# Last layer of a four-layer graph network: inverse roots computed between the statistics of other blocks, the last five roots on ScalarE, and two blocks of edge counts loaded one layer ahead

## The chip, the cores and the metric

The kernel runs on one core of one Trainium2 chip. The metric is device time in microseconds (us); the median of several runs is compared. A profile of one execution is shown beside the times. In it PE is TensorE (matmul), PEld its weight loads, DVE is VectorE, ACT is ScalarE, POOL is GpSimd, and SP is SyncE, the engine that issues most DMAs here.

## The reference, cut to what matters

Four graph layers run one after the other over the same 3125 nodes with 128 features and 103125 edges. After each layer the result is added to its input and normalised over the features.

```python
x = _layernorm(x + _L0_gnn_ref(...))   # weighted sum over the edges, relu
x = _layernorm(x + _L1_gnn_ref(...))   # attention with four heads
x = _layernorm(x + _L2_gnn_ref(...))   # attention with softmax
x = _layernorm(x + _L3_gnn_ref(...))   # this one, below

agg = segment_sum(x[src], dst) / maximum(deg, 1)
h   = relu(agg @ w1_l + b1 + x @ w1_r)              # 128 -> 256
agg = segment_sum(h[src], dst) / maximum(deg, 1)
y   = sigmoid(agg @ w2_l + b2 + h @ w2_r)           # 256 -> 128

def _layernorm(x, eps=1e-5):
    m = mean(x); v = var(x)
    return (x - m) / sqrt(v + eps)
```

## The kernel before, in words

The nodes are laid out as 25 blocks of 128 (`NB = 25`, `P = 128`, `NP = 3200`). The edges have been turned into a dense matrix of counts in DRAM, `ctd`: 25 row blocks of 128 x 3200 bf16, 800 KB each. A segment sum is then a product of this matrix with the features, and the kernel streams the row blocks from DRAM and multiplies.

A scheduler in the framework sets the order of instructions on each engine from their dependencies and from the order in the program. A tile pool that is opened takes the addresses of pools closed before it, and its first writers wait for the readers of those. DVE and ACT work on the last stage is an exception: it stands in a `manual_schedule` block, where these two engines keep the order of the program. SP's queue is in order, so a DMA whose wait is not met holds those behind it.

**Layer 2** runs over two groups of blocks (`QG`, 13 and 12) and, in each, over the 25 row blocks; `scores(q, c)` loads a strip of counts into `ct2` (three buffers), multiplies, takes the exponential on ACT and multiplies by the counts on DVE. The pool `p3` is opened before layer 2 and stays open through layer 3. It holds `f_rdeg`, `f_rdr`, the tile `f_ct0` (row block 0 of the counts, which layer 3 needs first) and the inputs of layer 3's products, `ip0` to `ip6`. The load of `f_ct0` (L1429) is written in the program at step 12 of the second group; the scheduler has put it on SP's queue behind the first three loads of layer 2.

**Layer 3** has two passes over the counts. The first (L1486) takes row blocks 0 to 19 from `ct0` or from `counts(b)`, a pool of six buffers filled on SP (L1477), then the last five blocks per 512 columns with the dense products between. The second pass (`add2`, L1562) keeps eight accumulators in PSUM, one for each group of output blocks:

```python
GT = [(0, 4), (4, 4), (8, 4), (12, 4), (16, 4), (20, 2), (22, 2), (24, 1)]
```

Its last five row blocks are multiplied group by group, so that group 0 is complete first and group 7 last. Each complete group g then goes through these steps:

- `sigmoid(g)`: DVE scales each block's accumulator and adds the own term (L1580, one instruction per block), ACT takes the sigmoid of the whole group (L1583).
- `moments(g)`: DVE adds the layer's input (L1588, one instruction per group), then one `bn_stats` (L1591) and one `bn_aggr` (L1593) per block give mean and variance in `mv`.
- `normal(b0, n)`: DVE computes 1/sqrt(var + eps) for n blocks with thirteen small instructions, each fed by the one before it: `var`, `half`, `sd` (L1598 to L1602), three Newton steps of three instructions (L1605 to L1607), and `ms` (L1609). ACT then writes the n normalised blocks (L1615), and SP stores them (L1619, L1621 for the 53 rows of the last block).

`normal` is called for blocks 0 to 7 after the sigmoid of group 2, for 8 to 15 after group 4, for 16 to 19 after group 5, and for 20 to 24 at the end, where two of the five blocks are written by DVE (L1613).

Of the kernel before, what the change touches and what calls it, by code (L numbers as in the profile page):

```python
# [7 lines left out]
F32 = mybir.dt.float32  # L8
BF16 = mybir.dt.bfloat16
I32 = mybir.dt.int32  # L10
AF = mybir.ActivationFunctionType
OP = mybir.AluOpType
# [3 lines left out]
P = 128  # L16
N = 3125
NB = 25
NP = NB * P
# [11 lines left out]
EPS = 1e-5  # L31
# [472 lines left out]
GT = [(0, 4), (4, 4), (8, 4), (12, 4), (16, 4), (20, 2), (22, 2), (24, 1)]  # L504
# [4 lines left out]
def fast_path(  # L509
# [4 lines left out]
    nc = tc.nc  # L514
# [3 lines left out]
    ctd = dram.tile([NB, P, NP], BF16, name="f_ctd")  # L518
# [8 lines left out]
    x = cst.tile([P, NB, P], F32, name="f_x")  # L527
    deg = cst.tile([P, NB], F32, name="f_deg")
# [118 lines left out]
    for g in range(NG):  # L647
        eg = ep.tile([P, EW // 16, 3, 16], F32, name="eg", bufs=3)
        nc.gpsimd.indirect_dma_start(
            out=eg.rearrange("p a t k -> p (a t k)"), out_offset=None, in_=td,  # L650
# [204 lines left out]
    for b in range(NBT):  # L855
        ohd, ohc, wod, _ = cur
# [49 lines left out]
    r = xw  # L906
# [9 lines left out]
    lp = ctx.enter_context(tc.tile_pool(name="f_p12", bufs=1))  # L916
# [14 lines left out]
    def step():  # L931

        todo = [f for k, f in due if k <= now[0]]
        due[:] = [(k, f) for k, f in due if k > now[0]]
        for f in todo:
            f()
        now[0] += 1
# [115 lines left out]
    with ExitStack() as st:  # L1053
# [239 lines left out]
        for x_, (g, hp, c) in enumerate(items):  # L1293
            i0, n = IG[g]
# [29 lines left out]
    p3 = ctx.enter_context(tc.tile_pool(name="f_p3", bufs=1))  # L1324
    rdeg = p3.tile([P, NB], F32, name="f_rdeg")
    rdr = p3.tile([P, NP], F32, name="f_rdr")
    ct0 = p3.tile([P, NP], BF16, name="f_ct0")
    ips = {}

    def in_parts(lp, g, i):  # L1330
# [6 lines left out]
    scale = float(P) ** -0.5  # L1337
    with ExitStack() as st:
# [13 lines left out]
        def degrees():  # L1352

            nc.vector.tensor_scalar(rdeg, deg, 1.0, None, OP.max)
            nc.vector.reciprocal(rdeg, rdeg)
            rd_ = dram.tile([NB, P], F32, name="rd_")
            t = bank()
            nc.tensor.transpose(t[0:NB, 0:P], rdeg, ident)
            rt = l2.tile([NB, P], F32, name="rt")
            nc.scalar.copy(rt, t[0:NB, 0:P])  # L1360
            nc.sync.dma_start(rd_, rt)
            nc.sync.dma_start(rdr, bass.AP(tensor=rd_.tensor, offset=rd_.offset, ap=[[0, P], [1, NP]]))
# [58 lines left out]
        for x_, (q, c) in enumerate(items):  # L1421
            i0, n = QG[q]
            if c == 0:
                acc = [ap.tile([P, 512], F32, name=f"acc2_{k}") for k in range((n + 2) // 3)]
            step()
            if (q, c) == (0, 3):
                degrees()
            if (q, c) == (1, 12):
                nc.sync.dma_start(ct0, ctd[0])  # L1429
            if q == 0 and NB - 4 <= c < NB - 1:  # L1430
                a = split + (c - NB + 4) * 512
                turned_y(a, min(512, N - a))
            if x_ + 1 < len(items):
                scores(*items[x_ + 1])
            if c < NB - 2:
                for k in range(n):
                    products2(acc, q, c, k)
            elif c == NB - 1:
                for k0 in range(0, n, 3):
                    m = min(3, n - k0)  # L1440
                    for b in (NB - 2, NB - 1):
                        for k in range(k0, k0 + m):
                            products2(acc, q, b, k)
                for k0 in range(0, n, 3):
                    m = min(3, n - k0)
                    t = acc[k0 // 3][:, 0 : m * (P + 1)].rearrange("p (b d) -> p b d", d=P + 1)
                    z = cp.tile([P, 3], F32, name="z2")
                    nc.vector.tensor_scalar(z[:, 0:m], t[:, :, P], 1e-38, None, OP.max)
                    nc.vector.reciprocal(z[:, 0:m], z[:, 0:m])
                    for j in range(m):  # L1450
                        b = i0 + k0 + j
                        nc.vector.scalar_tensor_tensor(
                            r[:, b, :], t[:, j, 0:P], z[:, j : j + 1], x[:, b, :], OP.mult, OP.add
                        )
                finish2(q)
# [5 lines left out]
    with ExitStack() as st:  # L1461
        fp = st.enter_context(tc.tile_pool(name="f_fp3", bufs=1))
        cp = st.enter_context(tc.tile_pool(name="f_cp3", bufs=HB + 1))
        lp = st.enter_context(tc.tile_pool(name="f_lp3", bufs=2))
# [6 lines left out]
        for g in range(3, len(GB)):  # L1471
            b0, n = GB[g]
            ips[g] = in_parts(lp, g, x[:, b0 : b0 + n, :])

        def counts(b):
            ct = cp.tile([P, NP], BF16, name="ct3")
            nc.sync.dma_start(ct, ctd[b])  # L1477
            return ct
# [11 lines left out]
            return done  # L1490

        for b in range(NB - HB):
            ct = counts(b) if b else ct0
            for k in range(len(CN)):
                done = add1(ct, b, k)
            if 3 <= b < 17 and b % 2:
                with tc.issue_after(done.ins):
                    turned(ps, xT, *GB[(b - 3) // 2])
            if b == 18:

                sd = fp.tile([P, 1], F32, name="f_sumdeg")
                nc.vector.tensor_reduce(sd, deg, AX.X, OP.add)
                t = ps.tile([P, 512], F32, name="tr")
                nc.tensor.matmul(t[:, 0:1], ones, sd, start=True, stop=True)
                nc.vector.tensor_scalar(good[:, 2:3], t[:, 0:1], float(E), None, OP.is_equal)
                nc.vector.tensor_tensor(good[:, 3:4], good[:, 0:1], good[:, 1:2], OP.mult)
                nc.vector.tensor_tensor(good[:, 3:4], good[:, 3:4], good[:, 2:3], OP.mult)
                nc.vector.tensor_copy(flag, good[0:1, 3:4])
# [32 lines left out]
        for k in range(K + 3):  # L1541
            if k < K:
                for b in range(NB - HB, NB):
                    add1(last[b], b, k)
                c, n = CN[k]
# [22 lines left out]
        for b in range(NB - HB):  # L1568
            ct = counts(b)
# [3 lines left out]
        mv = fp.tile([P, NB, 2], F32, name="mv3")  # L1573
        sg = {}

        def sigmoid(g):
# [6 lines left out]
            nc.scalar.activation(t, t, AF.Sigmoid)  # L1583
            sg[g] = t

        def moments(g):
            b0, n = GT[g]
            nc.vector.tensor_tensor(r[:, b0 : b0 + n, :], sg[g], x[:, b0 : b0 + n, :], OP.add)  # L1588
            bs = lp.tile([P, 4, 6], F32, name="bs3")
            for j in range(n):  # L1590
                nc.vector.bn_stats(bs[:, j, :], r[:, b0 + j, :])  # L1591
            for j in range(n):
                nc.vector.bn_aggr(mv[:, b0 + j, :], bs[:, j, :])  # L1593

        def normal(b0, n, by_v=()):

            va = lp.tile([P, 8], F32, name="var3")[:, 0:n]
            nc.vector.tensor_scalar(va, mv[:, b0 : b0 + n, 1], EPS, None, OP.add)  # L1598
            half = lp.tile([P, 8], I32, name="half3")[:, 0:n]
            nc.vector.tensor_scalar(half, va.bitcast(I32), 1, None, OP.arith_shift_right)  # L1600
            sd = lp.tile([P, 8], F32, name="sd3")[:, 0:n]
            nc.vector.tensor_scalar(sd.bitcast(I32), half, -1.0, float(0x5F3759DF), OP.mult, OP.add)  # L1602
            t = lp.tile([P, 8], F32, name="newton")[:, 0:n]
            for _ in range(3):
                nc.vector.tensor_tensor(t, sd, sd, OP.mult)  # L1605
                nc.vector.scalar_tensor_tensor(t, t, -0.5, va, OP.mult, OP.mult)
                nc.vector.scalar_tensor_tensor(sd, t, 1.5, sd, OP.add, OP.mult)  # L1607
            ms = lp.tile([P, 8], F32, name="ms3")[:, 0:n]
            nc.vector.scalar_tensor_tensor(ms, mv[:, b0 : b0 + n, 0], -1.0, sd, OP.mult, OP.mult)  # L1609
            for j in range(n):  # L1610
                b = b0 + j
                if b in by_v:
                    nc.vector.tensor_scalar(x[:, b, :], r[:, b, :], sd[:, j : j + 1], ms[:, j : j + 1], OP.mult, OP.add)  # L1613
                else:
                    nc.scalar.activation(  # L1615
                        x[:, b, :], r[:, b, :], AF.Identity, bias=ms[:, j : j + 1], scale=sd[:, j : j + 1]
                    )
            m = min(n, NF - b0)
            nc.sync.dma_start(out[b0 * P : (b0 + m) * P, :].rearrange("(b p) d -> p b d", p=P), x[:, b0 : b0 + m, :])  # L1619
            if m < n:  # L1620
                nc.sync.dma_start(out[NF * P : N, :], x[0:NR, NF, :])  # L1621

        with tc.manual_schedule(engines={mybir.EngineType.DVE, mybir.EngineType.Activation}):
            for g in range(len(GT)):
                for b in range(NB - HB, NB):
                    add2(last[b], b, g)
                sigmoid(g)
                if g == 2:
                    normal(0, 8)
                elif g == 4:  # L1630
                    normal(8, 8)
                elif g == 5:
                    normal(16, 4)
                moments(g)
            normal(20, 5, (NB - 2, NB - 1))


@with_exitstack
# [39 lines left out]
```

## Time and profile before

| | |
|---|---|
| median of 3 runs | 1528.68 us (1528.14 to 1530.35) |
| the profiled execution, whole | 1528.75 us |
| its span in the profile | 1526.9 us |
| PE busy | 1391.9 us (91%) |
| DVE busy | 985.8 us (65%) |
| ACT busy | 910.6 us (60%) |
| last matmul ends | about 1505.2 us |
| last ACT instruction ends | about 1521.0 us |

The page of a profile shows, in its section 2, the busy share of each engine in 40 slices of the span, a digit for each slice: 9 is 90% or more. The timeline lists instructions in order of time: start, duration, engine, line of the program, operation, tiles, shapes and count; neighbours of one line are merged, and a bracket gives idle time before the instruction and what ended it. The table by windows gives the busy time of each engine in a stretch, the granted clock of TensorE, the mean busy share of the 16 DMA engines and the GB/s that they moved.

### The profile page before, as it was taken

To read this page: it belongs to the slowest core of one execution; us is meant where nothing else is said; L and a number is where in the kernel's file an instruction comes from. 1 tells how busy PE (TensorE), PEld (TensorE's weight loads), DVE (VectorE), ACT (ScalarE), POOL (GpSimd) and SP (SyncE) were. 2 spreads that over 40 slices of the span, in tenths; PEclk is the share of its full clock that TensorE was granted. 3 is DMA by queue.
4 is the path that set the end of the run, shared out by engine and by line. 5 is a ranking of instruction groups with operands and counts; after the bars stand their busy time and mean duration, and the time that the engine had idled before them with its cause. 6 is when DMAs were issued, how large, how long until landed. Compare 5 with 4: busy or idle time off the path is not lost. (4 is left out here: it accounts for less than half of the span.)

```text
span 1526.9 us, 35224 instructions
## 1 busy us (share of the span) xinstructions
PE 1391.9 (91%) x14858; PEld 1220.9 (80%) x14871; DVE 985.8 (65%) x1608; ACT 910.6 (60%) x1865; POOL 126.8 (8%) x162
## 2 busy tenths in 40 slices
PE   4899999999997987899989989899999999999994
PEld 3898999998997876889979979677777764458994
DVE  4999899999990489879978888544464451012006
ACT  2988778888882479878778677554465431023003
POOL 2000000000000023203212311300000000000000
PEclk9999999999998999999999999999999999999997
DMA  6387787887878633444434433332222227503551
GB/s 193 88 216 212 208 228 206 236 211 208 222 211 247 207 96 99 145 123 122 129 121 116 130 89 104 101 111 68 73 64 80 69 89 259 200 22 151 196 174 45
DMA packets 210337, 223.92 MB, mean 147 GB/s; under 512 B 72860, under 2 KB 183975, under 8 KB 209913
## 3 DMA queue, kind: packets, MB, share of 16 engines
q1 hardware_dynamic: 206312, 217.26, 48.4%
q10 hardware_dynamic: 3457, 2.35, 0.6%
q8 instruction: 118, 1.93, 0.5%
q0 software_dynamic: 400, 1.97, 0.4%
q14 instruction: 50, 0.41, 0.1%
HBM read 157.19 MB, written 64.36 MB: 145 GB/s over the span
## 5 line engine op out<-in xcount | busy, mean ns | idle before, releaser
L1244 PE MATMUL acc<-vp,cm 128*128 128x198 bf16 x2500 | 344.5, 252 | 6.6 <-DVE cm L1229 4.1
L1228 ACT ACTIVATE fm<-adr,bas 128x896 bf16<-128x896 f32 (+1 forms) x320 | 286.2, 952 | 67.9 <-DVE cm L1229 63.3
L1239 PE MATMUL acc<-vp,ct 128*128 128x204 bf16 x1250 | 315.2, 256 | 9.7 <-DVE vp L1147 5.6
L1244 PEld LDWEIGHTS <-cm 128*128 128x128 bf16 x2500 | 235.8, 98 | 25.9 <-issue 10.4
L875 PE MATMUL wp<-wod,ohc 128*128 128x128 bf16 x3840 | 244.1, 219 | 8.8 <-ACT cs L880 6.6
L875 PEld LDWEIGHTS <-ohc 128*128 128x128 bf16 x3840 | 224.0, 98 | 9.8 <-issue 9.4
L836 DVE TENSOR_TENSOR wod<-ohd,w 128x4096 bf16<-128x4096 bf16 (+1 forms) x120 | 224.9, 1926 | 0.6 <-PE wp L875 0.6
L1229 DVE TENSOR_TENSOR cm<-fm,ct 128x896 bf16<-128x896 bf16 (+1 forms) x320 | 197.5, 647 | 36.3 <-PE acc L1244 13.2
L845 ACT ACTIVATE wod<-ohd,wu 128x128 bf16<-128x128 bf16 x640 | 197.0, 400 | 0.0
L1384 DVE TENSOR_TENSOR e<-e,ct 128x416 f32<-128x416 f32 (+1 forms) x175 | 108.2, 625 | 106.5 <-ACT e L1383 98.6
L1383 ACT ACTIVATE e<-s,f_nm 128x416 f32<-128x416 f32 (+1 forms) x175 | 109.5, 632 | 98.1 <-PE s L1380 90.8
L1388 PEld LDWEIGHTS acc<-self__8127,e 128*128 128x128 f32 x1250 | 148.4, 193 | 20.6 <-issue 18.8
L1388 PE MATMUL acc<-self__8127,e 128*128 128x129 f32 x1250 | 148.8, 276 | 0.5 <-DVE e L1384 0.5
L1380 PE MATMUL s<-yT,f_xT 128*128 128x416 f32 (+1 forms) x350 | 142.8, 543 | 4.6 <-ACT rt L1360 4.0
L797 PE MATMUL acc<-f_xw,cw 128*128 128x128 f32 x1000 | 119.8, 280 | 7.2 <-DMA cw<-wd 7.2
L1239 PEld LDWEIGHTS <-ct 128*128 128x128 bf16 x1250 | 122.5, 98 | 2.5 <-issue 1.5
L886 ACT COPY ws<-wp 128x512 f32<-128x512 f32 x160 | 93.5, 584 | 49.9 <-PE wp L875 48.3
L797 PEld LDWEIGHTS acc<-f_xw,cw 128*128 128x128 f32 x1000 | 116.3, 196 | 7.5 <-DMA cw<-wd 7.3
L867 PE MATMUL cp<-ohc,ohd 128*128 128x125 bf16 x1280 | 96.8, 218 | 21.0 <-ACT ws L886 17.4
L1380 PEld LDWEIGHTS s<-yT,f_xT 128*128 128x128 f32 x350 | 62.2, 191 | 55.5 <-issue 39.2
L827 DVE TENSOR_TENSOR ohd<-kd,ramp 128x4096 bf16<-128x4096 bf16 x40 | 91.4, 2286 | 21.2 <-PE cp L867 21.1
L1562 PEld LDWEIGHTS <-ct 128*128 128x128 bf16 x1875 | 104.9, 98 | 0.0
(292 smaller groups left out, 1490.3 us busy)
## 6 DMA issues: line engine op xcount, KB each, us to landing
ct<-f_ctd SPq DMA_DIRECT2D x49, 800.0 KB
wd<-ws SPq DMA_DIRECT2D x40, 896.0 KB
ct<-f_ctd SPq DMA_DIRECT2D x150, 224.0 KB
cw<-wd SPq DMA_DIRECT2D x50, 640.0 KB
f_ctd<-cs SPq DMA_DIRECT2D x20, 1000.0 KB
ct<-f_ctd SPq DMA_DIRECT2D x25, 416.0 KB
ct<-f_ctd SPq DMA_DIRECT2D x25, 365.2 KB
cw<-wd SPq DMA_DIRECT2D x25, 320.0 KB
```

Of the source, the lines that this page charges most:

```text
L797: nc.tensor.matmul(accs[j // 4][:, j % 4, :], cw[:, j - h, :], xw[:, i, :], start=False, stop=(i == NB - 1 and (j % 4 == 3 or j == n - 1)) ...
L836: nc.vector.tensor_tensor(f[:, 0:n].rearrange("p w (a t) -> p w a t", t=2), ohd[:, 0:n].rearrange("p w (a t) -> p w a t", t=2), twos(w2[s] ...
L845: nc.scalar.activation(wod[2][:, BW + w, :], ohd[:, BW + w, :], AF.Copy, scale=w3[:, 1, at : at + 1])
L875: nc.tensor.matmul(wp[:, j, :], ohc[:, w, :], wod[s][:, w, :], start=(j == 0 and q == 0 and s == 0), stop=(j == 3 and q == 1 and s == 2), ...
L1228: nc.scalar.activation(f[:, : n * P], at, AF.Relu, bias=bas[:, c, h : h + 1], scale=UP)
L1229: nc.vector.tensor_tensor(m[:, : n * P], f[:, : n * P], ct[:, : n * P], OP.min)
L1239: nc.tensor.matmul(out_(F1, PW), ct[:, k * P : (k + 1) * P], vp[:, c, hp : hp + 2, :, 2 * F1 : V1], start=(c == 0), stop=False, skip_group ...
L1244: nc.tensor.matmul(out_(0, 2 * F1)[:, j], ms[j][:, k * P : (k + 1) * P], vp[:, c, hp + j, :, 0 : 2 * F1], start=False, stop=(c == NB - 1 a ...
L1380: nc.tensor.matmul(s[:, :m], xT[:, c * P : (c + 1) * P], yT[:, i0 * P + a : i0 * P + a + m], start=True, stop=True)
L1383: nc.scalar.activation(e[:, a : a + m], s[:, :m], AF.Exp, bias=nm[:, q : q + 1], scale=scale)
L1384: nc.vector.tensor_tensor(e[:, a : a + m], e[:, a : a + m], ct[:, a : a + m], OP.mult)
L1388: nc.tensor.matmul(acc[k // 3][:, (k % 3) * (P + 1) : (k % 3 + 1) * (P + 1)], es[q, c][:, k * P : (k + 1) * P], vo[:, c, 0 : P + 1], start ...
```

## The change

At the start of layer 3, row blocks 0 and 1 of the counts have a tile of their own in `p3` (6,400 bytes more in each partition), both loaded at the place where block 0 was loaded; `counts(b)` is used from block 2 on.

At the end of layer 3, `normal` is cut into a list of small instructions (`roots`), the writing of the blocks (`scaled`) and the store (`store`). `moments` gives back a list too, and its first addition has become `total`. The function `mixed` issues the lists in turns, one instruction from each. The first four instructions of `roots` stand ahead of `total(g)`; the other nine are mixed with `moments(g)`. The roots of blocks 16 to 19 are taken beside group 6 instead of group 5. ACT's writing of blocks is cut into portions of four or two blocks, each placed behind the sigmoid of a later group. For the last five blocks ACT takes the square root and DVE its reciprocal; a square root of one column of `deg`, whose result nobody reads, stands ahead of it. Blocks 16 to 19 are written by DVE there.

```diff
-    ct0 = p3.tile([P, NP], BF16, name="f_ct0")
+    ct0 = [p3.tile([P, NP], BF16, name=f"f_ct0_{b}") for b in range(2)]
...
             if (q, c) == (1, 12):
-                nc.sync.dma_start(ct0, ctd[0])
+                for b in range(2):
+                    nc.sync.dma_start(ct0[b], ctd[b])
...
-            ct = counts(b) if b else ct0
+            ct = counts(b) if b > 1 else ct0[b]
...
+        def total(g):
+            b0, n = GT[g]
+            nc.vector.tensor_tensor(r[:, b0 : b0 + n, :], sg[g], x[:, b0 : b0 + n, :], OP.add)
+
         def moments(g):
             b0, n = GT[g]
-            nc.vector.tensor_tensor(r[:, b0 : b0 + n, :], sg[g], x[:, b0 : b0 + n, :], OP.add)
             bs = lp.tile([P, 4, 6], F32, name="bs3")
+            return [
+                lambda j=j: nc.vector.bn_stats(bs[:, j, :], r[:, b0 + j, :]) for j in range(n)
+            ] + [lambda j=j: nc.vector.bn_aggr(mv[:, b0 + j, :], bs[:, j, :]) for j in range(n)]
...
+        def roots(b0, n):
...
+            return [
+                lambda: nc.vector.tensor_scalar(va, mv[:, b0 : b0 + n, 1], EPS, None, OP.add),
+                lambda: nc.vector.tensor_scalar(half, va.bitcast(I32), 1, None, OP.arith_shift_right),
+                lambda: nc.vector.tensor_scalar(sd.bitcast(I32), half, -1.0, float(0x5F3759DF), OP.mult, OP.add),
+            ] + [
+                lambda: nc.vector.tensor_tensor(t, sd, sd, OP.mult),
+                lambda: nc.vector.scalar_tensor_tensor(t, t, -0.5, va, OP.mult, OP.mult),
+                lambda: nc.vector.scalar_tensor_tensor(sd, t, 1.5, sd, OP.add, OP.mult),
+            ] * 3 + [
+                lambda: nc.vector.scalar_tensor_tensor(ms, mv[:, b0 : b0 + n, 0], -1.0, sd, OP.mult, OP.mult),
+            ]
+
+        def scaled(b0, n, on_v=False):
+            for b in range(b0, b0 + n):
+                sd, ms = by[b]
+                if on_v:
+                    nc.vector.tensor_scalar(x[:, b, :], r[:, b, :], sd, ms, OP.mult, OP.add)
                 else:
+                    nc.scalar.activation(x[:, b, :], r[:, b, :], AF.Identity, bias=ms, scale=sd)
...
+        def mixed(*lists):
+
+            for k in range(max(len(l) for l in lists)):
+                for l in lists:
+                    if k < len(l):
+                        l[k]()
...
                 sigmoid(g)
                 if g == 2:
-                    normal(0, 8)
+                    chain = roots(0, 8)
+                elif g == 3:
+                    scaled(0, 4)
                 elif g == 4:
-                    normal(8, 8)
+                    chain = roots(8, 8)
+                    scaled(4, 4)
+                    store(0, 8)
                 elif g == 5:
-                    normal(16, 4)
-                moments(g)
-            normal(20, 5, (NB - 2, NB - 1))
+                    scaled(8, 4)
+                elif g == 6:
+                    chain = roots(16, 4)
+                    scaled(12, 2)
+                mixed(chain[:4])
+                total(g)
+                mixed(moments(g), chain[4:])
+                chain = []
+            n = 5
+            va = some("var3", n)
+            sd = some("sd3", n)
+
+            nc.scalar.activation(some("root3", 1), deg[:, 0:1], AF.Sqrt)
+            scaled(14, 2)
+            store(8, 8)
+            nc.vector.tensor_scalar(va, mv[:, 20:25, 1], EPS, None, OP.add)
+            nc.scalar.activation(sd, va, AF.Sqrt)
+            scaled(16, 4, True)
+            store(16, 4)
+            nc.vector.reciprocal(sd, sd)
+            ms = some("ms3", n)
+            nc.vector.scalar_tensor_tensor(ms, mv[:, 20:25, 0], -1.0, sd, OP.mult, OP.mult)
...
+            scaled(20, 3)
+            scaled(23, 2, True)
+            store(20, 5)
```

More of the change, by code (lines that the diff above doesn't have):

```diff
@@ L1584, in sigmoid @@
             sg[g] = t
+        def total(g):
+            b0, n = GT[g]
+            nc.vector.tensor_tensor(r[:, b0 : b0 + n, :], sg[g], x[:, b0 : b0 + n, :], OP.add)
         def moments(g):
             b0, n = GT[g]
-            nc.vector.tensor_tensor(r[:, b0 : b0 + n, :], sg[g], x[:, b0 : b0 + n, :], OP.add)
             bs = lp.tile([P, 4, 6], F32, name="bs3")
-            for j in range(n):
-                nc.vector.bn_stats(bs[:, j, :], r[:, b0 + j, :])
-            for j in range(n):
-                nc.vector.bn_aggr(mv[:, b0 + j, :], bs[:, j, :])
@@ L1595, in normal @@
[L1595 to L1613, printed above, removed]
-                else:
-                    nc.scalar.activation(
-                        x[:, b, :], r[:, b, :], AF.Identity, bias=ms[:, j : j + 1], scale=sd[:, j : j + 1]
-                    )
@@ new lines, in moments, with some @@
+            return [
+                lambda j=j: nc.vector.bn_stats(bs[:, j, :], r[:, b0 + j, :]) for j in range(n)
+            ] + [lambda j=j: nc.vector.bn_aggr(mv[:, b0 + j, :], bs[:, j, :]) for j in range(n)]
+        def some(name, n, d=F32):
+            return lp.tile([P, 8], d, name=name)[:, 0:n]
+        def roots(b0, n):
+            va = some("var3", n)
+            half = some("half3", n, I32)
+            sd = some("sd3", n)
+            t = some("newton", n)
+            ms = some("ms3", n)
+            for j in range(n):
+                by[b0 + j] = sd[:, j : j + 1], ms[:, j : j + 1]
+            return [
[9 more added lines that the diff above has]
+            ]
@@ L1618, in normal, with store @@
+        def scaled(b0, n, on_v=False):
[3 more added lines that the diff above has]
+                    nc.vector.tensor_scalar(x[:, b, :], r[:, b, :], sd, ms, OP.mult, OP.add)
+                else:
+                    nc.scalar.activation(x[:, b, :], r[:, b, :], AF.Identity, bias=ms, scale=sd)
+        def store(b0, n):
             m = min(n, NF - b0)
-            nc.sync.dma_start(out[b0 * P : (b0 + m) * P, :].rearrange("(b p) d -> p b d", p=P), x[:, b0 : b0 + m, :])
@@ L1620, in normal @@
             if m < n:
                 nc.sync.dma_start(out[NF * P : N, :], x[0:NR, NF, :])
+            nc.sync.dma_start(out[b0 * P : (b0 + m) * P, :].rearrange("(b p) d -> p b d", p=P), x[:, b0 : b0 + m, :])
+        def mixed(*lists):
[3 more added lines that the diff above has]
+                        l[k]()
+        by = {}
+        chain = []
         with tc.manual_schedule(engines={mybir.EngineType.DVE, mybir.EngineType.Activation}):
@@ L1628, in fast_path @@
                 if g == 2:
-                    normal(0, 8)
+                    chain = roots(0, 8)
+                elif g == 3:
+                    scaled(0, 4)
                 elif g == 4:
-                    normal(8, 8)
+                    chain = roots(8, 8)
+                    scaled(4, 4)
+                    store(0, 8)
                 elif g == 5:
-                    normal(16, 4)
-                moments(g)
-            normal(20, 5, (NB - 2, NB - 1))
+                    scaled(8, 4)
[5 more added lines that the diff above has]
+                mixed(moments(g), chain[4:])
+                chain = []
+            n = 5
+            va = some("var3", n)
+            sd = some("sd3", n)
+            nc.scalar.activation(some("root3", 1), deg[:, 0:1], AF.Sqrt)
[6 more added lines that the diff above has]
+            nc.vector.reciprocal(sd, sd)
+            ms = some("ms3", n)
+            nc.vector.scalar_tensor_tensor(ms, mv[:, 20:25, 0], -1.0, sd, OP.mult, OP.mult)
+            for j in range(n):
+                by[20 + j] = sd[:, j : j + 1], ms[:, j : j + 1]
+            scaled(20, 3)
+            scaled(23, 2, True)
+            store(20, 5)
 @with_exitstack
```

## The prediction

> **What bounds the kernel now.** I read the page's slices first, then the timeline of the end, then that of layer 3's start, then the DMA windows of the last stores. The slices (PE, DVE, ACT):
>
> ```profile
> PE   4899999999997987899989989899999999999994
> DVE  4999899999990489879978888544464451012006
> ACT  2988778888882479878778677554465431023003
> ```
>
> PE sets the time up to the last slice. In that slice (38 us) its digit is 4 and DVE's is 6: a tail without matmuls. The chain of waits says the same: from 1487.67 us on it is DVE and ACT. The timeline of the tail, for groups 2 and 3 and for the last roots:
>
> ```profile
> 1495.88 0.17 DVE L1598 TENSOR_SCALAR var<-mv 128x8 f32<-128x8 f32 x1
> 1496.08 0.17 DVE L1600 TENSOR_SCALAR half<-var 128x8 int32<-128x8 int32 x1
> ...
> 1498.29 0.17 DVE L1609 SCALAR_TENSOR_TENSOR ms<-mv,sd 128x8 f32<-128x8 f32 x1
> 1498.38 0.69 DVE L1588 TENSOR_TENSOR f_xw<-t,f_x 128x512 f32<-128x512 f32 x1
> 1499.10 0.87 DVE L1591 BATCH_NORM_STATS2 bs<-f_xw 128x6 f32<-128x128 f32 x4
> 1499.89 0.36 DVE L1593 BATCH_NORM_AGGREGATE mv<-bs 128x2 f32<-128x6 f32 x4
> 1500.16 1.09 DVE L1580 SCALAR_TENSOR_TENSOR t<-acc,f_rdeg,self__8127 128x128 f32<-128x128 f32 x4
> ...
> 1517.16 0.17 DVE L1598 TENSOR_SCALAR var<-mv 128x5 f32<-128x5 f32 x1
> ...
> 1519.77 1.26 ACT L1615 ACTIVATE f_x<-f_xw,ms,sd 128x128 f32<-128x128 f32 x3 [3.52 <-DVE ms L1609]
> ```
>
> A small instruction that needs the one before it starts 0.20 us after it (1495.88 to 1496.08). One that doesn't starts 0.09 us after it (1498.29 to 1498.38). So thirteen dependent ones take 12 x 0.20 + 0.09 = 2.49 us in which DVE does little. At the end of layer 2, DVE already runs such instructions beside statistics of other blocks:
>
> ```profile
> 1248.51 0.16 DVE L1448 TENSOR_SCALAR z<-acc 128x3 f32<-128x3 f32 x1
> 1248.59 0.28 DVE L765 BATCH_NORM_STATS2 bs<-f_xw 128x6 f32<-128x128 f32 x1
> 1248.79 0.16 DVE L1449 RECIPROCAL z<-z 128x3 f32<-128x3 f32 x1
> ```
>
> The statistic starts 0.08 after the small one, and the next small one, which needs the first, 0.20 after the statistic: **a pair costs 0.28 us** where apart it costs 0.20 + 0.20 = 0.40. At the start of layer 3:
>
> ```profile
> 1252.68 4.12 PE L1486 MATMUL acc<-f_ct,ip 128*128 128x512 bf16 x20 [1.52 <-issue]
> 1257.73 4.55 PE L1486 MATMUL acc<-ct,ip 128*128 128x512 bf16 x23 [0.93 <-issue]
> ```
>
> PE ends row block 0 at 1256.80 and waits 0.93 us for block 1, whose load was issued at 1252.70, when DVE's last L1452 let go of layer 2's buffers. No such gap follows for block 2. The final store, by windows of 1 us (last two figures: DMA share, GB/s):
>
> ```profile
> 1522.00:1523.00 1.00, 0.00 (x0) 0.00 (x0) 0.00 (x0) 0.00 (x0) 0.00 (x0) 0.50 0.93 272
> 1523.00:1524.00 1.00, 0.00 (x0) 0.00 (x0) 0.00 (x0) 0.00 (x0) 0.00 (x0) 0.50 0.05 13
> ```
>
> It is issued at 1521.06; its 256 KB move from about 1521.97 to 1523.0, and the span ends 3.9 us later. The 512 KB store issued at 1501.70 moved from 1502.65 to 1504.48. So stores start 0.95 us after issue and fill the DMA engines at 280 to 292 GB/s.
>
> **What the Trainium skill says.** "VectorE: DVE Perf Modes", section "The DRAIN you can't avoid", says that the next DVE instruction waits until the pipe is empty and that a semaphore between two adds nothing. The trace differs for small ones: 0.09 us without a dependence, 0.20 with one. I use the trace. "ScalarE: Activation LUTs", section "What ACT_TABLE_LOAD costs", gives 1.283 us for a load plus 1.38 of drain. The trace has the 1.283, but the drain isn't seen:
>
> ```profile
> 989.67 1.28 ACT L969 ACT_TABLE_LOAD   x1 [6.07 <-DVE sd L968]
> 990.96 0.21 ACT L969 ACTIVATE sd<-sd 128x7 f32<-128x7 f32 x1
> ```
>
> so I charge 1.30 us. Its section "Table sets: the hidden batching unit" says that identity lies in every set; the trace has L978's identities at 974.12 between exponentials with no load, so ACT's `scaled` brings none. "DMA: Bandwidth & Descriptors", section "Issuing engines are not separate DMA queues", says that all DMAs share the same 16 engines; here all stores come from SP anyway, and what counts is their sum.
>
> **The change, step by step**, on the clock of the execution before; layer 3's start is added at the end.
>
> Groups 0 and 1: unchanged; group 2's L1580 still starts at 1494.87. *Group 2*: `var` 1495.88, then three steps of 0.20 and one of 0.09 allow `total` at 1496.58; the sigmoid (ends 1496.69) sets it at 1496.72. Statistics 0.72 later, at 1497.44. Then four pairs of 0.28 (1.12), four pairs of a `bn_aggr` (0.07 apart alone) with a dependent step, 0.20 each (0.80), and the last step and what follows, 0.21: group 3 starts at 1499.57 instead of 1500.16, **0.59 won**. *Group 3*: its sigmoid waited for eight identities of ACT (0.28 idle in the chain); now they follow it, so it takes group 1's 3.58 instead of 3.87: **0.29 won**. *Group 4*: as group 2, **0.59**. *Groups 5 and 6*: before 6.21 us together (1509.32 to 1515.53). Now 5 has no chain: L1580 to `total` 1.08, to the end 1.08. 6: `var` after 0.49, `total` 0.69 later, statistics 0.45, two pairs of 0.28, two of `bn_aggr` 0.20 and the rest of the chain 1.01: together 5.76, **0.45 won**. So group 7 starts 1.92 earlier, at 1513.61, and its sigmoid ends at 1514.33. ACT's portions of four (1.6 us) end before the next sigmoid is due in each case.
>
> *The last roots.* ACT: table load to 1515.63, the unread root to 1515.76 (a short ACTIVATE lets the next one start 0.12 after it, 990.96 to 991.08), two identities of 0.386, so the real root starts at 1516.53; its `var` has been ready since about 1515.4, so ACT, not DVE, is the bound. Root 0.21, reciprocal and `ms` 0.45, three identities 1.26: ACT ends at 1518.45, before at 1521.03. **2.58 won**. DVE's four blocks (4 x 0.26) run from 1515.3 to 1516.4, beside ACT; if DVE were late they would stand ahead of the reciprocal.
>
> *The stores.* These are moved, and here part is given back. Blocks 8 to 15 (512 KB) were stored from about 1510.8 on; now SP issues them only when ACT has written block 15, at 1516.62. Blocks 16 to 19 (256 KB), before at 1514.04, follow at 1517.0; then the small one and the last 256 KB at 1518.5, behind them in the same queue. In all 1050 KB start moving at 1517.57 and at 292 GB/s take 3.6: they end at 1521.2 (1521.3 at 280), where the last store alone would have ended at 1520.45. Before: 1523.0. So **1.8 won** of the 2.58.
>
> *Layer 3's start.* Block 1 lies ready, so the 0.93 goes. Late next would be block 2: it takes the first load of 1252.70, which landed by 1257.7, and is needed at 1256.80 + 4.2 = 1261.0. PE is busy 99.6% of 1300 to 1400 and without a break to 1505, so all of it reaches the tail: **0.93 won** (bounds 0 to 0.93). The cost: one more DMA on SP, 0.4 us, behind the three loads at 962.99 and ahead of the fourth, which waits until 972.08 anyway. Its 800 KB take 2.0 to 2.5 us at the 326 to 394 GB/s moved there, and the DMA share was down to 0.19 at 970 to 972. The target lies where layer 1's values lay, released like block 0's. Cost nil, hidden by that SP wait; both ends below.
>
> Sum: 1.8 + 0.93 = 2.75. The profiled execution, 1528.75, is 0.07 above the median, and its span leaves 1.85 outside, unchanged. From the median, **1525.9 us**, -0.18%.
>
> **The rivals.** (B) *The stores don't bind*: with the end following ACT's last identity, the gain is 2.58 + 0.93 = 3.5, **1525.2**. For it: nothing else moves at that time, and pairs may cost less than 0.28. Against: the store windows show the engines full at 292 GB/s. (C) *The change doesn't do what it says*: if statistics and steps don't overlap, four pairs cost 0.12 more each, four of the others 0.07: 0.76 for groups 2 and 4, 0.38 for group 6, 1.9 in all, leaving 0.85: **1527.8**. Against it stand the rows of layer 2. (D) *Slower: the added load blocks SP.* The queue is in order. If block 1's tile is released late (for instance with layer 1's last normalisation, at 990.96), the fourth load of layer 2 stands behind it. That load's counts are multiplied at 985.66, and it needs some 2.2 us to land (0.95 to start, 1.2 for 416 KB at 350 GB/s), so from about 983 on each us costs one; beyond 989 the kernel is slower by over 0.2%. At 991 it is +8, net **1534**. Against it: block 0's tile, beside it, was free at 962.97. An order of layer 2 shifted by the scheduler belongs here too, between nothing and 3 us either way.
>
> **How the numbers follow.** Forecast 0.45, B 0.33, C 0.13, D 0.09. A measurement of this kernel can tell about 0.2%, 3.06 us, from no change: below 1525.6. The forecast's own range is 1525.2 to 1526.7 (rate of the stores, one tenth per group, runs that differ by 0.5), half of it beyond (0.23); of B nearly all (0.30). Faster 0.53, same 0.22 + 0.03 + 0.13 = 0.38, slower 0.09. The range, 1524.4 to 1528.0, holds the forecast, B with 0.8 below it, and C; it leaves out D and some tails.
>
> **What would show it.** Block 1 at about 1256.8 without idle time before it. Group 7's L1580 2.85 us earlier, small steps 0.28 apart beside `bn_stats`. One table load right after the last sigmoid. A DMA share near 1 without a hole from about 1516.6 to 1520.3. Wrong if the steps stay 0.40 apart in pairs (C), if the share falls before the last store is issued (B), or if layer 3 starts later than 1252.7 (D).

## The result, and the profile after

The changed kernel takes 1525.53 us (median of 22 runs, 1524.67 to 1527.61); the kernel before, in 22 runs, 1528.71 us. The ratio is 0.9981, with a 95% interval of 0.9974 to 0.9987. The profiled execution took 1526.18 us, with a span of 1524.3.

Executions differ by up to 3 us in the layers ahead of the change: over the twelve profiles of this document layer 3's first product starts between 1252.05 and 1255.21 us (1252.68 before, 1252.82 after). So I measure the stage from that product (the first matmul into `acc` from `f_ct`) to the end of the span. That is 1526.9 - 1252.68 = **274.2 us before** and 1524.3 - 1252.82 = **271.5 us after**, 2.7 less.

The slices of the page after (PE, DVE, ACT) look as before at the end, since 2.7 us are a fourteenth of one slice (38 us):

```profile
PE   4899999999997987899989989899999999999994
DVE  4999999999991389869978878534464351012006
ACT  2988778888883479878778777454465331023003
```

The start of layer 3, from the timeline of PE (start, duration, engine, line, count at the end of the line):

```profile
1252.82 8.08 PE L1487 MATMUL acc<-f_ct,ip 128*128 128x512 bf16 x42 [1.52 <-issue]
1260.74 8.08 PE L1487 MATMUL acc<-ct,ip 128*128 128x512 bf16 x42
```

Both preloaded blocks are now one line of 42 matmuls with no idle time noted inside, and the first block from the pool follows at 1260.74. Two blocks take 7.92 us, 3.96 each. Before, block 1 started 5.05 us after block 0.

The tail, groups 2 and 3, from the timeline of DVE:

```profile
1494.94 0.16 DVE L1611 TENSOR_SCALAR var<-mv 128x8 f32<-128x8 f32 x1
...
1495.78 0.69 DVE L1589 TENSOR_TENSOR f_xw<-t,f_x 128x512 f32<-128x512 f32 x1
1496.50 0.29 DVE L1595 BATCH_NORM_STATS2 bs<-f_xw 128x6 f32<-128x128 f32 x1
1496.71 0.15 DVE L1616 SCALAR_TENSOR_TENSOR newton<-newton,var 128x8 f32<-128x8 f32 x1
1496.78 0.29 DVE L1595 BATCH_NORM_STATS2 bs<-f_xw 128x6 f32<-128x128 f32 x1
1496.98 0.15 DVE L1617 SCALAR_TENSOR_TENSOR sd<-newton,sd 128x8 f32<-128x8 f32 x1
...
1497.59 0.18 DVE L1596 BATCH_NORM_AGGREGATE mv<-bs 128x2 f32<-128x6 f32 x1
1497.71 0.17 DVE L1617 SCALAR_TENSOR_TENSOR sd<-newton,sd 128x8 f32<-128x8 f32 x1
1497.79 0.17 DVE L1596 BATCH_NORM_AGGREGATE mv<-bs 128x2 f32<-128x6 f32 x1
...
1498.51 0.17 DVE L1619 SCALAR_TENSOR_TENSOR ms<-mv,sd 128x8 f32<-128x8 f32 x1
1498.60 1.12 DVE L1581 SCALAR_TENSOR_TENSOR t<-acc,f_rdeg,self__8127 128x128 f32<-128x128 f32 x4
```

A Newton step beside a `bn_stats` now follows the last one after 0.27 us (1496.71 to 1496.98), beside a `bn_aggr` after 0.20. From `var` to the next group's scaling it is 3.66 us, where it was 4.28.

The end, from the timeline of all engines:

```profile
1513.14 0.31 ACT L1584 ACTIVATE t<-t 128x128 f32<-128x128 f32 x1 [2.13 <-DVE t L1581]
1513.47 1.28 ACT L1671 ACT_TABLE_LOAD   x1
...
1514.76 0.20 ACT L1671 ACTIVATE root<-f_deg 128x1 f32<-128x1 f32 x1
1514.87 0.86 ACT L1628 ACTIVATE f_x<-f_xw,ms,sd 128x128 f32<-128x128 f32 x2
1515.64 0.19 ACT L1675 ACTIVATE sd<-var 128x5 f32<-128x5 f32 x1
...
1516.29 1.26 ACT L1628 ACTIVATE f_x<-f_xw,ms,sd 128x128 f32<-128x128 f32 x3 [0.46 <-DVE ms L1680]
...
1516.92 0.26 SPq L1633 DMA_DIRECT2D out_dram<-f_x  x1
1517.57 0.87 SPq L1634 DMA_DIRECT2D out_dram<-f_x  x1
```

The table load follows the last sigmoid at once. The root that counts starts only at 1515.64, behind the load, the unread root and two identities, although its `var` was ready at 1514.5. SP issues the store of blocks 16 to 19 (256 KB) at 1515.57, when DVE has written the last of them, and that of blocks 8 to 15 (512 KB) behind it at 1516.06: the scheduler has turned the order of the program round. The last store is issued at 1517.57. And the DMA engines, by windows of 1 us (the last two figures are DMA share and GB/s):

```profile
1516.00:1517.00 1.00, 0.00 (x0) 0.00 (x0) 0.82 (x4) 0.71 (x2) 0.00 (x0) 0.50 0.47 124
1517.00:1518.00 1.00, 0.00 (x0) 0.00 (x0) 0.00 (x0) 0.55 (x2) 0.00 (x0) 0.50 1.02 293
1518.00:1519.00 1.00, 0.00 (x0) 0.00 (x0) 0.00 (x0) 0.00 (x0) 0.00 (x0) 0.50 1.01 280
1519.00:1520.00 1.00, 0.00 (x0) 0.00 (x0) 0.00 (x0) 0.00 (x0) 0.00 (x0) 0.50 1.03 288
1520.00:1521.00 1.00, 0.00 (x0) 0.00 (x0) 0.00 (x0) 0.00 (x0) 0.00 (x0) 0.50 0.34 96
```

They are full from 1516.5 to about 1520.3 without a hole. The last store was issued at 1517.57, when about 508 KB of those ahead of it had not begun to move; its bytes could have been gone by about 1519.5 (an estimate), had it been alone (1521.06 to 1523.0 before). A few packets come late: the last of all ends at 1521.86 (1523.20 before). From the issue of the last store to the end of the span it is 6.7 us now and was 5.8 before.

What fills this time is SP's own path. After its last store SP reads a flag that decides whether a fallback has to run (`values_load`, then `tc.If`), branches, and then checks the semaphores of its DMAs. The rows of SP in the views of these lines (shortest, median and longest in ns, then the first and last start in us), before:

```profile
L1645 SPq TENSOR_LOAD <-flag x1: 490/490/490, 1521.5 to 1521.5; - x1
...
L1646 SPq EVENT_SEMAPHORE  x8: 17/17/17, 1524.7 to 1525.2; - x8
...
L1646 SPq COMPARE_BRANCH  x1: 50/50/50, 1522.0 to 1522.0; - x1
```

and after:

```profile
L1695 SPq TENSOR_LOAD <-flag x1: 782/782/782, 1518.5 to 1518.5; - x1
...
L1696 SPq EVENT_SEMAPHORE  x8: 17/17/17, 1522.1 to 1522.6; - x8
...
L1696 SPq COMPARE_BRANCH  x1: 50/50/50, 1519.4 to 1519.4; - x1
```

SP took 0.38 us to issue the last store before and 0.87 after, and 0.49 and 0.78 to read the flag. From the branch to SP's next instruction 2.57 and 2.66 us pass, and from there to the end 2.23 in both. The differences, 0.49 + 0.29 + 0.09, are the 0.9. The eight checks take 17 ns each and are through in half a microsecond in both, so no store holds them up. The span therefore does not end a fixed time after the last packet (3.7 us before, 2.4 after). It ends when SP is through, and SP is slower while many bytes are queued.

### The profile page after: what moved, and what is told of

Its sections match the earlier page's. It is cut to its first block, busy times and chain, and to the rows that moved or that the text cites. A ratio compares the mean times of both kernels' runs of the same rounds, so it can differ in the third digit from the quotient of the medians.

```text
span 1524.3 us, 35229 instructions
## 1 busy us (share of the span) xinstructions
PE 1394.6 (91%) x14871; PEld 1221.3 (80%) x14871; DVE 984.4 (65%) x1602; ACT 911.2 (60%) x1864; POOL 127.3 (8%) x162
```

## The experiments

In each, "stage" is the time from layer 3's first product to the end of the span of the profiled execution, and "tail" the time from the first group's scaling on DVE (L1580 or L1581) to the last group's: 27.86 us before, 25.97 after. Ratios are to the kernel before, with 95% intervals.

### 1. The preloaded blocks alone

```diff
 (kernel before)
-    ct0 = p3.tile([P, NP], BF16, name="f_ct0")
+    ct0 = [p3.tile([P, NP], BF16, name=f"f_ct0_{b}") for b in range(2)]
...
+                for b in range(2):
+                    nc.sync.dma_start(ct0[b], ctd[b])
...
-            ct = counts(b) if b else ct0
+            ct = counts(b) if b > 1 else ct0[b]
```

> The kernel before, with the two preloaded blocks of counts and nothing else. Measured from layer 3's first product to the end of the span, before takes 274.2 us and the changed kernel 271.5. My theory: only PE's wait for block 1 goes, 0.93 to 1.1 us, the tail keeps its 27.9 us from the first group's L1580 to the last group's: 273.1 from layer 3's first product, about 1527.7 in all. Rival: the wait only moves to block 2, whose load is now the first one in the queue: 274.2, no change.

Measured: stage 1528.3 - 1255.21 = 273.1 us, tail 27.86; median 1527.53, ratio 0.9987 (0.9981 to 0.9994). The wait did not move to block 2: PE's line of the two preloaded blocks takes 7.92 us here too, and the next follows at once. The tail is untouched. The part is worth 1.1 us.

### 2. The tail alone

```diff
 (changed kernel, with one preloaded block)
-            ct = counts(b) if b > 1 else ct0[b]
+            ct = counts(b) if b else ct0
```

> The changed kernel with one preloaded block, as before: the edits of the tail alone. My theory: the two parts add up, so PE waits for block 1 again (0.93 to 1.1 us) and the tail keeps its gain: 26.0 us from the first group's L1580 to the last group's, 272.6 from layer 3's first product to the end of the span, about 1526.7. Rival: the tail's gain needs the earlier start, because the stores are late either way: 273.5 or more.

Measured: stage 1525.6 - 1253.09 = 272.5, tail 25.98; median 1526.85, ratio 0.9987 (0.9981 to 0.9994). The two parts add to within 0.1: 1.1 of the first and 1.7 here against the 2.7 of both.

### 3. Statistics and steps one after another

```diff
-                mixed(moments(g), chain[4:])
+                mixed(moments(g))
+                mixed(chain[4:])
```

> The changed kernel with the statistics of a group first and the nine remaining steps of the roots after them, instead of in turns. My theory: a dependent step then costs 0.20 us beside nothing: 0.66 us more in groups 2 and 4 and 0.34 in group 6, so 27.6 us instead of 26.0 from the first group's L1580 to the last group's, and the end 1.7 later: 273.2 from layer 3's first product. Rival: the overlap is worth little and the gain of the tail came from the four steps ahead of the addition and from ACT's smaller portions: 26.0 to 26.3 us and 271.5 to 271.8.

Measured: stage 1526.6 - 1253.48 = 273.1, tail 27.55; ratio 0.9989 (0.9981 to 0.9997). The tail is 1.58 us longer. So the turns are worth 1.6 us, of the 1.9 that the tail up to the last group had gained.

### 4. Without the root that nobody reads

```diff
-            nc.scalar.activation(some("root3", 1), deg[:, 0:1], AF.Sqrt)
```

> The changed kernel without the square root that nobody reads. ACT then writes blocks 14 and 15 before it loads the table, not after. My theory: the sum on ACT is the same less 0.12 us, so its last identity ends within 0.2 us of where it did, but the store of blocks 8 to 15 is issued 1.3 to 1.4 us earlier, the queue of stores is shorter, and the end comes 0.8 to 1.0 us sooner: 270.5 to 270.7 from layer 3's first product. Rival: the end follows ACT's last identity and the queue of stores doesn't matter: 271.3 to 271.5.

The timeline of this kernel's end:

```profile
1512.49 0.31 ACT L1584 ACTIVATE t<-t 128x128 f32<-128x128 f32 x1 [2.12 <-DVE t L1581]
1512.70 0.86 ACT L1628 ACTIVATE f_x<-f_xw,ms,sd 128x128 f32<-128x128 f32 x2
...
1513.95 1.28 ACT L1674 ACT_TABLE_LOAD   x1 [0.39 <-DVE var L1673]
1515.24 0.21 ACT L1674 ACTIVATE sd<-var 128x5 f32<-128x5 f32 x1
...
1517.20 0.38 SPq L1634 DMA_DIRECT2D out_dram<-f_x  x1
```

Half a miss. The load did not run while ACT was free: it waited 0.39 us for `var`. Here a wait for `var` stands as an instruction of its own (L1674, 17 ns at 1513.9) ahead of the load. So ACT's last identity ends 4.37 us after the last sigmoid instead of 4.10, which I had not foreseen: the unread root does have a use. All the same the stage is 1523.1 - 1252.19 = 270.9, 0.6 **shorter**, with ACT 0.27 later. The store of blocks 8 to 15 goes out at 1513.59, 0.8 after the sigmoid and not 2.6 after it, so that only some 46 KB are left ahead of the last store. SP issues that one in 0.38 us, and from there to the end it is 5.9 us again. That speaks for the queue of stores, and against ACT's last identity alone, as what sets the end. The median, 1525.63 (ratio 0.9979, 0.9972 to 0.9985), can't tell this from the changed kernel.

### 5. The store of blocks 8 to 15 in two

```diff
                     scaled(12, 2)
+                    store(8, 6)
...
-            store(8, 8)
+            store(14, 2)
```

> The changed kernel with the store of blocks 8 to 15 in two: 8 to 13 as soon as ACT has written block 13 (beside group 6), 14 and 15 where all eight were stored. No engine's work changes; SP issues one DMA more. My theory: with 384 KB of 1050 KB gone from the queue at the end, the last store no longer stands behind others, and the end comes 0.7 to 0.9 us sooner: 270.6 to 270.8 us from layer 3's first product to the end of the span (changed kernel 271.5). Rival: the end follows ACT's last identity, which stays: 271.4 to 271.6.

The DMA windows of its end:

```profile
1518.00:1519.00 1.00, 0.00 (x0) 0.00 (x0) 0.00 (x0) 0.61 (x2) 0.00 (x0) 0.50 0.95 271
1519.00:1520.00 1.00, 0.00 (x0) 0.00 (x0) 0.00 (x0) 0.00 (x0) 0.00 (x0) 0.50 0.46 138
1520.00:1521.00 1.00, 0.00 (x0) 0.00 (x0) 0.00 (x0) 0.00 (x0) 0.00 (x0) 0.50 0.61 170
```

There is a hole now: the queue runs dry before the last store, issued at 1518.63 with some 111 KB ahead of it, begins. The stage is 1524.4 - 1253.86 = 270.5, and ACT's last identity still ends 4.10 us after the last sigmoid. With the work of DVE and ACT unchanged, the end comes 0.9 us sooner. SP issues the last store in 0.38 us and reads the flag in 0.49 again, and from that issue to the end it is 5.8 us. This is the 0.9 that the changed kernel's queue of stores costs, and it shows that the queue is what slows SP. Ratio 0.9977 (0.9967 to 0.9988, 8 runs).

### 6. Newton steps for the last five roots

```diff
-            nc.scalar.activation(some("root3", 1), deg[:, 0:1], AF.Sqrt)
             scaled(14, 2)
             store(8, 8)
...
-            scaled(16, 4, True)
+            scaled(16, 4)
             store(16, 4)
...
+            mixed(roots(20, 5))
             scaled(20, 3)
             scaled(23, 2, True)
```

> The changed kernel with Newton steps on DVE for the last five roots too, one after another, no square root and no table load on ACT, and blocks 16 to 19 written by ACT. DVE's thirteen steps take 2.6 us, so ACT's last identity ends 4.8 us after the last sigmoid instead of 4.1. My theory: ACT writes blocks 14 and 15 at once, their store is issued 1.4 us earlier, and the shorter queue of stores pays for the later identity: 271.2 to 271.5 from layer 3's first product, no change to the changed kernel's 271.5. Rival: the end follows ACT's last identity: 272.1 to 272.2.

Measured: ACT's last identity ends 4.85 us after the last sigmoid, 0.75 later than in the changed kernel; the stage is 1526.0 - 1254.59 = 271.4, the same. In the changed kernel as it stands, the part with ScalarE's root brings nothing: from the last group's scaling to the issue of the last store it wins 0.76 us, and from there to the end it loses 0.79 (6.72 against 5.93), because ACT loads a table before it writes blocks 14 and 15 and their store is late. The experiment also gives blocks 16 to 19 back to ACT, so it weighs the whole part and not the root alone. (Median 1527.02, ratio 0.9986, 0.9978 to 0.9994; the medians alone don't settle this.)

### 7, 9 and 10. Another order at the end

```diff
-                    scaled(12, 2)
+                    scaled(12, 4)
+                    store(8, 8)
                 mixed(chain[:4])
+                if g == 7:
+                    scaled(16, 1, True)
                 total(g)
...
             nc.scalar.activation(some("root3", 1), deg[:, 0:1], AF.Sqrt)
-            scaled(14, 2)
-            store(8, 8)
             nc.vector.tensor_scalar(va, mv[:, 20:25, 1], EPS, None, OP.add)
             nc.scalar.activation(sd, va, AF.Sqrt)
-            scaled(16, 4, True)
-            store(16, 4)
+            scaled(17, 2, True)
             nc.vector.reciprocal(sd, sd)
+            scaled(19, 1, True)
+            store(16, 4)
...
-            scaled(20, 3)
-            scaled(23, 2, True)
+            scaled(20, 2)
+            scaled(22, 3, True)
```

> The changed kernel with another order at the end: ACT writes blocks 12 to 15 together beside group 6 and SP stores 8 to 15 there; DVE writes block 16 while it waits for the last sigmoid, 17 and 18 before the reciprocal, 19 after it, and three of the last five blocks (ACT two). My theory: the square root starts when its table is there, 0.75 us sooner, and no store waits for another: the last store's bytes end 1.9 us sooner, 269.6 from layer 3's first product, about 1523.8 in all. Rival: only ACT's end counts, which comes 1.0 us sooner: 270.4.

Measured: stage 1521.8 - 1252.05 = 269.8, tail 25.96; ratio 0.9979 (0.9970 to 0.9987). The stage came out as expected, but the medians, 1526.0 here and 1525.53 for the changed kernel on another occasion, hid it. So both kernels ran once more, on one chip:

> The changed kernel as it is, beside the reordered one on the same chip. My theory: 271.5 us from layer 3's first product to the end of the span, 2.7 less than the kernel before, and a median about 2.7 to 3.2 below it. Rival: part of the gain in the runs was chance in the earlier layers: 271.5, but a median only 1 to 2 below.

> The reordered kernel once more, beside the changed one. My theory: 269.7 to 269.8 us from layer 3's first product to the end, 1.7 less than the changed kernel, and a median 1 to 2 us below its. Rival: runs differ by more than that from their earlier layers, so that the medians tell nothing though the tail is shorter.

Measured: the changed kernel has a stage of 1524.6 - 1253.14 = 271.5, median 1526.78, ratio 0.9983 (0.9976 to 0.9989); the reordered one 1523.0 - 1253.17 = 269.8, median 1525.16 (8 runs), ratio 0.9973 (0.9963 to 0.9984). The medians differ by 1.6 us, the stages by 1.6 to 1.7; the intervals of the ratios overlap, so it is the traces that carry this. In them about 0.7 of the gain lies ahead of the issue of the last store and about 0.9 behind it (5.8 us to the end, with 174 KB ahead of that store). The reordered kernel's end, in the second of its runs:

```profile
1515.09 0.20 ACT L1674 ACTIVATE root<-f_deg 128x1 f32<-128x1 f32 x1
1515.20 0.19 ACT L1676 ACTIVATE sd<-var 128x5 f32<-128x5 f32 x1
1515.94 0.88 ACT L1628 ACTIVATE f_x<-f_xw,ms,sd 128x128 f32<-128x128 f32 x2 [0.56 <-DVE ms L1682]
```

The root that counts follows the unread one at once.

### 8. ACT's writing in portions of eight

```diff
                 elif g == 3:
-                    scaled(0, 4)
...
                 mixed(moments(g), chain[4:])
                 chain = []
+                if g == 2:
+                    scaled(0, 8)
+                    store(0, 8)
+                elif g == 4:
+                    scaled(8, 8)
+                    store(8, 8)
```

> The changed kernel with ACT's writing in portions of eight again, ahead of the next group's sigmoid, and stored there. My theory: since the roots in turns with the statistics are ready only when the next group's L1581 starts, eight identities (3.2 us) now stand in front of that group's sigmoid: group 3's comes 2.0 us later and group 5's 2.6, so 30.6 us from the first group's L1581 to the last group's (26.0 in the changed kernel) and about 275 us from layer 3's first product to the end. Rival: the portions are worth no more than the 0.28 us idle that the kernel before showed, once for each group of eight: 26.6 us and 271.5 or less.

Its timeline behind group 2's roots:

```profile
1498.72 3.19 ACT L1628 ACTIVATE f_x<-f_xw,ms,sd 128x128 f32<-128x128 f32 x8 [2.96 <-DVE ms L1619]
1501.81 0.61 ACT L1584 ACTIVATE t<-t 128x512 f32<-128x512 f32 x1
...
1502.45 0.69 DVE L1589 TENSOR_TENSOR f_xw<-t,f_x 128x512 f32<-128x512 f32 x1 [2.74 <-ACT t L1584]
```

DVE stands idle for 2.74 us before group 3's addition and, by the same view, 3.04 before group 5's. Stage 1527.6 - 1252.83 = 274.8, tail 30.44; ratio 1.0000 (0.9992 to 1.0009). The whole gain is gone. The smaller portions are no side matter: taking the roots beside the statistics makes them ready when the next sigmoid is due, and only a later place for ACT's writing keeps the sigmoid in front.

## Why the prediction was right, point by point

The forecast was 1525.9 us, 2.75 less than before; the runs gave 3.2 less in one set and 2.7 in the other, the stage in the profile 2.7. The median of the first set, 1525.53, lies halfway between the forecast and rival B's 1525.2 and can't decide between them. The stage does: 271.5 us, where 274.2 less B's 3.5 would be 270.7.

| step | predicted | measured in the two profiles |
|---|---|---|
| start of layer 3 | 0.93 | 1.08 (first product to first group: 234.99, then 233.91) |
| group 2 | 0.59 | 0.62 (5.29, then 4.67) |
| group 3 | 0.29 | 0.20 (3.87, then 3.67) |
| group 4 | 0.59 | 0.63 (5.29, then 4.66) |
| groups 5 and 6 | 0.45 | 0.44 (6.21, then 5.77) |
| last group to ACT's end | 0.66 | 0.65 (5.50, then 4.85) |
| stores, given back | -0.78 | -0.89 (issue of the last to the end: 5.84, then 6.73) |
| sum | 2.73 | 2.73 |

The steps of the prediction add to 2.73; its sum says 2.75, which changes nothing.

- **Layer 3's start** was a little under-sized. I took the 0.93 us that the timeline noted as idle, from the end of the last matmul that it showed. Starts are the better measure: 5.05 us from block 0 to block 1 against 3.96 without a wait make 1.09. Experiment 1 shows the same 1.1, and in every profile with two preloaded blocks the first group comes 233.91 us after the first product.
- **The load beside it** did cost nothing. The DMA share at 970 to 972 us is 1.01 where it was 0.19, but SP's fourth load follows its first after 9.10 us (9.09 before) and DVE's first multiplication after 6.98 (6.96 before). Layer 2, from its first load to layer 3's first product, takes 289.69 us before and 289.53 after. Rival D did not happen.
- **Pairs of 0.28** were right to 0.01, and experiment 3 shows that they are 1.6 of the 1.9 us that the tail gained, against rival C. Experiment 8 shows that this gain also needs ACT's smaller portions. The prediction set its small instructions against "VectorE: DVE Perf Modes", section "The DRAIN you can't avoid"; that section also says that an instruction which is not held starts earlier, so the 0.09 us of an independent one do not contradict it. Group 3 won less than charged: its sigmoid starts 0.09 us after DVE's last scaling, where group 1's took 0.03.
- **The end** was read rightly from ACT: load, unread root, two identities, root, with no drain after the load (1.29 us from its start to the unread root's), as charged; the 0.3 of DVE's `reciprocal` waiting for ACT confirms that DVE was not the bound. "ScalarE: Activation LUTs", section "Table sets: the hidden batching unit", on identity holds too: no second load follows.
- **The stores** are the step that made the forecast: without it the end would have been put at 1525.2 (rival B). Its size was right, and experiments 4, 5 and 6, each by another way, show that a shorter queue brings the end nearer. Its path was not right. The prediction let the span end 3.9 us after the last byte, which was to come 2.73 us sooner (1.8 + 0.93). Measured from layer 3's first product, the last packet came only 1.5 us sooner, and the end follows SP, which was slower by 0.5 us at the last issue and by 0.3 at the flag. What SP does at and after its last store appears nowhere in the prediction. That its 0.8 us and the measured 0.9 agree is luck.

What is open: the start of layer 2 varies by more than 2 us between the profiled executions (962.49 to 964.84), and in one of them, experiment 1's, layer 2 itself took 1.4 us longer than in the others. So the 0.5 us between the two sets of medians has no cause that these runs show. Nor do they show why SP's instructions take longer while stores are queued.

## What to carry to other kernels

Short dependent instructions on DVE cost 0.20 us each here, and independent ones 0.09; put independent instructions between dependent ones, one in turn, and price the pair from rows where the program already does so. Then ask what each result triggers on the next engine and where that lands: here roots that come later push ACT's writing in front of a sigmoid unless it is cut and moved. At the end of a kernel, count the bytes of all stores issued in the last microseconds: here a store moved behind a table load cost as much as the shorter chain had won. And follow the engine that issues the last store to the end of the span; do not take the last byte for the end.

## What the runs showed of the hardware that I had not expected

- A table load doesn't always run ahead of its ACTIVATE's input. In experiment 4 it waited 0.39 us for `var`, behind a wait that is an instruction of its own ahead of the load (the load of L969 in the kernel before, which the prediction shows, had waited for its `sd` too, 6.07 us).
- SP took 0.85 to 0.87 us to issue the last store, and then 0.77 to 0.79 to read a flag, where about 507 KB of earlier stores had not begun to move (changed kernel, experiments 2, 3 and 9). In the other eight profiles, with 27 to 174 KB, it took 0.38 and 0.48 to 0.49.
- From SP's branch on the flag to its next instruction 2.5 to 2.7 us passed in all twelve profiles, and 2.23 from there to the end. The last packet of the stores ended 2.3 to 3.7 us before the end.
- The idle time noted in a timeline of matmuls understated a wait: 0.93 us noted, 1.09 by the starts.
